# Head of layer 2 in a four-layer graph network: the second batch's turn is queued behind the first batch's products, and the first batch's bias is added by VectorE

## The chip, the core and the metric

The kernel runs on one core of one Trainium2 chip. The metric is the device time of one execution in microseconds (us). TensorE (PE in the profile) multiplies matrices and turns (transposes) them through PSUM, PEld is its loading of weights, VectorE (DVE) and ScalarE (ACT) work elementwise, GpSimd (POOL) does small elementwise work and issues DMAs, and SyncE (SP) issues DMAs.

## The reference

A batch of 16 graphs, each with 1024 nodes and 128 features, goes through four graph layers. After every layer its output is added to the input and each row is normalised. The two lines that matter here are the end of layer 1 and the start of layer 2 (both cut):

```python
# layer 1 ends: h1, h2, h3 are its three batch-normalised hidden states, mf the node mask
xc = jnp.concatenate([h1, h2, h3], axis=-1) * mf[..., None]
y = (xc @ Wl + bl) * mf[..., None]
x = _layernorm(x + y, axis=-1)
# layer 2 begins
h = jnp.einsum('bnf,of->bno', x, W_w) + W_b
e = jnp.einsum('bil,bkl->bik', h @ A, h)
e = e + jnp.swapaxes(e, 1, 2)
att = jax.nn.softmax(jnp.where(adj > 0, e, 0), axis=1) * adj
h_prime = jax.nn.relu(jnp.einsum('bij,bjk->bik', att, h))
```

Layer 2 goes on with gates, a residual sum and a normalisation, and layer 3 is two graph convolutions.

## The kernel before

The program is one long list of tiles. Layers 0 and 1 are done for all batches; layer 1 runs over its batches three times, since its batch norm needs sums over all of them. The change lies where layer 1 has ended and layers 2 and 3 begin (lines 1546 to 1833). From there each batch is worked on in four generator functions: `before` ends layer 1 for this batch and prepares the operands of layer 2, `attention` does the scores, the softmax and the product with the hidden rows in eight steps, `mix` does the gates, and `convolve` does layer 3. A function `in_rounds` lets several of them take turns: each yields a number of rounds that it wants to pause. The first call runs `before` for batches 0 and 1 together, so these two make the head; after that round b runs `attention` of batch b beside `convolve` of b-2, `mix` of b-1 and `before` of b+1.

The order in which the Python code issues instructions isn't yet the order on the engines. A scheduler in the tile framework moves an instruction forward on its engine when it expects its inputs earlier. `keep_in_program_order` ties one instruction behind what was issued last on its engine. Each engine then takes its own queue strictly in order, and an instruction that waits holds up everything behind it on that engine. Buffers come from pools, and a buffer is free again when its last reader is done: `yT` has one buffer (`rows("yT")`), and the PSUM pool `ps_h` has two banks, used in turn by turns and products.

The steps of `before` for one batch, with the lines of the profile:

- L1639: GpSimd multiplies the mask by the bias row `blrow` (named l2A in the profile), 1024 columns wide, into `yT`. `blrow` is ready after L1240, the last step of layer 1's batch norm.
- L1644: TensorE sums the three products of the hidden states with `Wl` into PSUM (`py`).
- L1660: VectorE adds `yT` to each half of `py`, giving `yn`.
- L1664: VectorE adds `yn` to the residual rows `xn`, in two halves for the two batches of the head.
- L794, L796, L742, L745, L799, L801 (`normed`): the statistics on VectorE, the power -1/2 on GpSimd (`ln_rstd`), the shift on VectorE (`ln_nb`), and eight scalings of 128 columns on ScalarE, in two groups of four.
- L1669 with L759 (`turned`): TensorE turns the eight blocks of `xn`, ScalarE copies each half to `xT`.
- L1673 and L1677 with L766 (`products`): `hT` is W2T with `xT`, `G` is As2 with `hT`; each is two products of 512 columns, and ScalarE copies each half out.
- L1680 with L759: TensorE turns `hT`, VectorE copies each half to `hn`.

`attention` then makes scores from `G` and `hT` (L1706, and turned earlier scores at L1708), masks them on VectorE (L1711, `em`), takes the exponential on ScalarE (L1714, `ex`), and multiplies it with the scaled hidden rows `hs` on TensorE (L1694, `acc`).

On the engines of the kernel before, TensorE's queue holds, in this order: the sums of both batches, the turn of batch 0, the turn of batch 1, the four W2T products of both, the As2 products of batch 0, and then turns of hT, score products and the As2 products of batch 1 in alternation. On ScalarE both batches' scalings and xT copies stand ahead of all hT copies.

Of the kernel before, what the change touches and what calls it, by code (L numbers as in the profile page):

```python
# [17 lines left out]
OP = mybir.AluOpType  # L18
# [4 lines left out]
P = 128  # L23
# [616 lines left out]
def fast_kernel(ctx: ExitStack, tc: tile.TileContext, t: dict, out: bass.AP, flag: bass.AP):  # L640

    nc = tc.nc
    B, N, D = t["x"].shape
    NT = N // P
# [6 lines left out]
    identf = consts.tile([P, P], F32, name="identf")  # L651
# [18 lines left out]
    mf = consts.tile([P, BT], F32, name="mf")  # L670
# [57 lines left out]
    def tiles3(ap):  # L728
        return ap.rearrange("p (t d) -> p t d", d=P)

    def per_row(v):

        return v[:, :, None].to_broadcast([P, NT, P])

    def per_col(v):
        return v[:, None, :].to_broadcast([P, NT, P])
# [11 lines left out]
    def halves(psum, tag="h"):  # L748

        for h in range(H2):  # L750
            p = psum.tile([P, 512], F32, name="ph", tag=tag)
            yield p, slice(h * 512, (h + 1) * 512), range(h * 4, h * 4 + 4)

    def turned(psum, src, tag="h"):

        for p, c, blocks in halves(psum, tag):
            for i, k in enumerate(blocks):
                s = src[:, k, :] if len(src.shape) == 3 else src[:, k * P:(k + 1) * P]
                nc.tensor.transpose(p[:, i * P:(i + 1) * P], s, identf)  # L759
            yield p, c, slice(blocks[0], blocks[-1] + 1)  # L760

    def products(psum, *pairs, tag="h"):

        for p, c, _ in halves(psum, tag):
            for i, (W, x) in enumerate(pairs):
                nc.tensor.matmul(p, W, x[:, c], start=(i == 0), stop=(i == len(pairs) - 1))  # L766
            yield p, c
# [19 lines left out]
    def normed(small, r, fine=False, pieces=None):  # L787

        for k in pieces or spans(fine):
            n = k.stop - k.start  # L790
            st = small.tile([P, NT, 6], F32, name="ln_st")
            mv = small.tile([P, NT, 2], F32, name="ln_mv")
            for i in range(n):
                nc.vector.bn_stats(st[:, i, :], r[:, k.start + i, :])  # L794
            for i in range(n):
                nc.vector.bn_aggr(mv[:, i, :], st[:, i, :])  # L796
            rstd = power_mhalf(small, mv[:, :n, 1], add=LN_EPS, name="ln_rstd")
            nb = small.tile([P, NT], F32, name="ln_nb")
            nc.vector.scalar_tensor_tensor(nb[:, :n], mv[:, :n, 0], -1.0, rstd, op0=OP.mult, op1=OP.mult)  # L799
            for i in range(n):  # L800
                nc.scalar.activation(r[:, k.start + i, :], r[:, k.start + i, :], AF.Identity,  # L801
                                     scale=rstd[:, i:i + 1], bias=nb[:, i:i + 1])

    def spans(fine):

        return [slice(0, NT // 2), slice(NT // 2, NT)] if fine else [slice(0, NT)]
# [85 lines left out]
    ps_h = ending.enter_context(tc.tile_pool(name="l0_ph", bufs=2, space=PSUM, reuse_waits="tile"))  # L892

    with tc.tile_pool(name="l0_raw", bufs=1, side="right") as raw:
# [4 lines left out]
        p = ps_h.tile([P, P], F32, name="wtr", tag="h")  # L899
# [3 lines left out]
        p = ps_h.tile([P, P], F32, name="wtr", tag="h")  # L903
# [3 lines left out]
        p = ps_h.tile([P, 1], F32, name="wtr", tag="h")  # L907
# [14 lines left out]
    def before(s, b):  # L922
# [4 lines left out]
        for it in range(NT):  # L927
# [19 lines left out]
            if it == (2 if b else 0):  # L947
                s.xT = work.tile([P, N], F32, name="xT", bufs=2)
                for p, c, _ in turned(ps_h, s.xn):
                    nc.scalar.copy(s.xT[:, c], p)  # L950
# [69 lines left out]

    state = [Batch() for _ in range(B)]
    in_rounds([before(state[0], 0), chain([8], attention(state[0], 0)), chain([16], before(state[1], 1))])
    nc.vector.tensor_scalar(gbh, gb, 0.5, None, op0=OP.mult)
    for b in range(1, B):
        streams = []
        if b < B - 1:
            streams.append(before(state[b + 1], b + 1))
        streams.append(attention(state[b], b))
        if b:
            streams.append(after(state[b - 1], b - 1))  # L1030
        in_rounds(streams)
# [226 lines left out]
    with ExitStack() as ph:  # L1258
# [6 lines left out]
        ps_h = ph.enter_context(tc.tile_pool(name="l1_ph", bufs=4, space=PSUM, reuse_waits="tile"))  # L1265
# [49 lines left out]
        class Step:  # L1315


            def __init__(self, l, before):
                s = str(l + 1)
                self.l = l  # L1320
                self.Wr = matrix(wts, t[f"L1_gnn_Wr{s}"], "Wr", 2)
                self.Wx = matrix(wts, t[f"L1_gnn_Wx{s}"], "Wx", 2)
                self.brow = row_bcast(wts, t[f"L1_gnn_b{s}"], P, "b", 2)
                self.gcol = column(wts, t[f"L1_gnn_g{s}"], f"gcol{s}")
                self.becol = column(wts, t[f"L1_gnn_be{s}"], f"becol{s}")
                self.stats = wts.tile([P, B * H2, 6], F32, name="stats", bufs=2)
                self.batches = [Batch() for _ in range(B)]
                if before is not None:
                    for st, st0 in zip(self.batches, before.batches):
                        st.__dict__.update(st0.__dict__)  # L1330
# [225 lines left out]
    with ExitStack() as ph:  # L1556
# [3 lines left out]
        ps_h = ph.enter_context(tc.tile_pool(name="l2_ph", bufs=2, space=PSUM, reuse_waits="tile"))  # L1560
# [3 lines left out]
        W2T, b2, As2, gw, gb, nbig, blrow, Wl = l2.W2T, l2.b2, l2.As2, l2.gw, l2.gb, l2.nbig, l2.blrow, l2.Wl  # L1564
# [3 lines left out]
        def wide(name, bufs=1, dtype=F32):  # L1568
            return work.tile([P, N], dtype, name=name, bufs=bufs)

        def rows(name, bufs=1, dtype=F32):
            return work.tile([P, NT, P], dtype, name=name, bufs=bufs)
# [60 lines left out]
        def before(s, b):  # L1633

            if b:
                l2.load(s, b)
            yield 2
            yb = rows("yT")
            nc.gpsimd.tensor_tensor(yb, per_row(mf[:, b * NT:(b + 1) * NT]), per_col(blrow), op=OP.mult)  # L1639

            def summed(p, blocks, ls):
                for i, j in enumerate(blocks):
                    for l in ls:
                        nc.tensor.matmul(p[:, i * P:(i + 1) * P], s.hb[l][:, j * P:(j + 1) * P], Wl[:, l, :],  # L1644
                                         start=(l == 0 and (i % 4 == 0 or len(ls) == 3)), stop=(l == 2 and (i % 4 == 3 or len(ls) == 3)))

            if b < 2:

                p = ps_w.tile([P, N], F32, name="py", tag="w")
                for ls in ((0, 1), (2,)):  # L1650
                    summed(p, range(NT), ls)
                turns = [(p[:, h * 512:(h + 1) * 512], range(4 * h, 4 * h + 4)) for h in range(H2)]
            else:
                turns = ((p, blocks) for p, _, blocks in halves(ps_h))
            yn = rows("yn", 1)
            for p, blocks in turns:
                if b >= 2:
                    summed(p, blocks, range(3))
                k = slice(blocks[0], blocks[-1] + 1)
                nc.vector.tensor_add(yn[:, k, :], tiles3(p), yb[:, k, :])  # L1660
            yield 2

            for k in spans(b < 2):
                nc.vector.tensor_add(s.xn[:, k, :], s.xn[:, k, :], yn[:, k, :])  # L1664
            normed(small, s.xn, b < 2)
            yield 6
            s.xT = wide("xT", 2)
            for p, c, _ in turned(ps_h, s.xn):
                nc.scalar.copy(s.xT[:, c], p)  # L1669
            yield 1  # L1670
            s.hT = wide("hT", 2)
            for p, c in products(ps_h, (W2T, s.xT)):
                nc.scalar.activation(s.hT[:, c], p, AF.Identity, bias=b2)  # L1673
            yield 1
            s.G = wide("G", 2)
            for p, c in products(ps_h, (As2, s.hT)):
                nc.scalar.activation(s.G[:, c], p, AF.Copy, scale=-1.0)  # L1677
            s.hn = wide("hn", 2)
            for p, c, _ in turned(ps_h, s.hT):
                nc.vector.tensor_copy(s.hn[:, c], p)  # L1680
            yield
# [200 lines left out]
```

## Time and profile before

| what | value |
|---|---|
| median of 3 runs | 2661.71 us (2660.23 to 2662.22) |
| the profiled execution, its own time | 2657.81 us |
| its span, first to last instruction | 2656.1 us |
| TensorE busy in the span | 2509.0 us (94%) |
| VectorE, ScalarE, GpSimd busy | 2106.4, 1957.0, 356.3 us |
| mean granted TensorE clock | 0.984 of full speed |
| shares of the chain that ended last | PE 53%, DVE 19%, ACT 13%, issue 5%, POOL 4%, DMA 2% |
| L1639 (yT), GpSimd | 16 times, 1.89 us each at the median, first at 1624.2 |
| L1660 (yn), VectorE, halves of the head | 4 times, 0.68 us each |
| L1664 (xn), VectorE, halves of the head | 4 times, 0.68 to 2.38 us, mean 1.53 |
| L1711 (em), first of layer 2 | at 1659.61 |
| L1694 (acc), first of layer 2 | at 1663.79 |

The profile is of one execution. Its times count from the start of its span. A row of the timeline merges instructions of one group that follow each other: start, length from the first start to the last end, engine, line, tiles, count, and in brackets how long the engine was idle before it and what ended that. The ends of matmuls are modelled, about 0.17 us after the array has taken its last column, so busy time of TensorE is on the high side. A float32 product of 512 columns shows as two instructions. "PEclk" is the share of full speed that TensorE's clock was granted.

### The profile page before, as it was taken

To read this page: it belongs to the slowest core of one execution; us is meant where nothing else is said; L and a number is where in the kernel's file an instruction comes from. 1 tells how busy PE (TensorE), PEld (TensorE's weight loads), DVE (VectorE), ACT (ScalarE), POOL (GpSimd) and SP (SyncE) were. 2 spreads that over 40 slices of the span, in tenths; PEclk is the share of its full clock that TensorE was granted. 3 is DMA by queue.
4 is the path that set the end of the run, shared out by engine and by line. 5 is a ranking of instruction groups with operands and counts; after the bars stand their busy time and mean duration, and the time that the engine had idled before them with its cause. 6 is when DMAs were issued, how large, how long until landed. Compare 5 with 4: busy or idle time off the path is not lost.

```text
span 2656.1 us, 44982 instructions
## 1 busy us (share of the span) xinstructions
PE 2509.0 (94%) x16580; PEld 1838.7 (69%) x16584; DVE 2106.4 (79%) x5832; ACT 1957.0 (74%) x3141; POOL 356.3 (13%) x316
## 2 busy tenths in 40 slices
PE   7999999997888869999999998999999999999987
PEld 5777777675666648888888896566666666666655
DVE  5888888887899877777788875777888787887786
ACT  7898898886888866667656534777777777777774
POOL 0001111013000001111122133011111111111001
PEclk9999999998999989999999998999999999999998
DMA  5555555530000052224467582111222111111100
GB/s 195 177 171 176 167 167 183 168 113 21 2 3 2 2 214 96 96 96 146 156 241 249 198 291 105 40 48 65 74 87 70 64 64 64 64 64 64 48 25 26
DMA packets 110103, 285.72 MB, mean 108 GB/s; under 512 B 12080, under 2 KB 53168, under 8 KB 102704
## 3 DMA queue, kind: packets, MB, share of 16 engines
q1 hardware_dynamic: 88832, 197.17, 22.1%
q0 software_dynamic: 21040, 85.57, 9.1%
q8 instruction: 133, 2.18, 0.3%
q14 instruction: 98, 0.80, 0.1%
HBM read 202.85 MB, written 79.82 MB: 106 GB/s over the span
## 4 chain that ended last, share of the span: by engine, by line
PE 53%; DVE 19%; ACT 13%; issue 5%; POOL 4%; DMA 2%; POOLq 0%; ACTq 0%; DVEq 0%; SPq 0%
PE acc L1306 9%; PE ph L1628 8%; PE acc L1694 6%; PE ph L1440 5%; PE ph L759 3%; PE ph L1644 3%; PE acc L973 2%; PE pmm L1706 2%; PE pmm L724 2%; PE ph L1615 2%; ACT em L985 2%; PE ph L766 2%; ACT xn L801 2%; DVE mid L1096 2%; DVE keep L1147 2%
## 5 line engine op out<-in xcount | busy, mean ns | idle before, releaser
L973 PEld LDWEIGHTS acc<-hs,em 128*128 128x128 f32 x2048 | 250.2, 193 | 38.2 <-issue 27.0
L973 PE MATMUL acc<-hs,em 128*128 128x128 f32 x2048 | 270.6, 280 | 0.9 <-DVE hs L989 0.7
L1694 PE MATMUL acc<-ex,hs 128*128 128x512 f32 x512 | 250.3, 599 | 6.2 <-DVE hs L1721 4.1
L724 PE MATMUL pmm<-xT,G 128*128 128x512 f32 x512 | 251.4, 604 | 1.4 <-DVE mx L983 0.7
L801 ACT ACTIVATE xn<-xn,ln_nb,ln_rstd 128x128 f32<-128x128 f32 x512 | 204.8, 480 | 55.3 <-DVE ln_nb L799 55.3
L1306 PE MATMUL acc<-a,hi 128*128 128x512 f32 x768 | 235.0, 398 | 3.0 <-ACT hi L1272 3.0
L1306 PE MATMUL acc<-a,lo 128*128 128x512 f32 x768 | 228.3, 392 | 3.1 <-DVE lo L1273 3.1
L745 POOL TENSOR_TENSOR ln_rstd<-ln_rstd,mhalf 128x8 f32<-128x8 f32 (+1 forms) x69 | 107.9, 1564 | 806.1 <-DVE ln_rstd L742 452.2
L1714 ACT ACTIVATE ex<-em,mn 128x1024 f32<-128x1024 f32 x128 | 146.6, 1145 | 89.2 <-DVE mn L1711 85.9
L983 DVE CUSTOM_DVE_ANT_0 em<-pmm,msk 128x1024 f32<-128x1024 f32 x128 | 155.9, 1218 | 35.5 <-PE pmm L724 33.2
L985 ACT ACTIVATE em<-em,mx 128x1024 f32<-128x1024 f32 x128 | 146.0, 1141 | 48.0 <-DVE mx L983 46.4
L1706 PE MATMUL pmm<-G,hT 128*128 128x512 f32 (+3 forms) x416 | 171.4, 520 | 0.1
L1306 PEld LDWEIGHTS acc<-a,lo 128*128 128x128 f32 x768 | 142.9, 188 | 34.0 <-DVE lo L1273 4.5
L1306 PEld LDWEIGHTS acc<-a,hi 128*128 128x128 f32 x768 | 140.7, 188 | 33.6 <-ACT hi L1272 3.7
L1156 ACT ACTIVATE carry<-pc,negone 128x1024 fp8e4<-128x1024 f32 x128 | 141.4, 1116 | 27.0 <-PE pc L1155 24.3
L1711 DVE CUSTOM_DVE_ANT_0 em<-pmm,msk 128x1024 f32<-128x1024 f32 x128 | 155.2, 1213 | 2.3 <-PE pmm L1708 0.6
L931 ACT ACTIVATE carry<-an 128x1024 fp8e4<-128x1024 f32 x128 | 134.1, 1049 | 24.5 <-DMA an<-in_adj 23.7
L980 ACT ACTIVATE msk<-carry,l0nbig 128x1024 bf16<-128x1024 fp8e4 x128 | 145.9, 1139 | 0.0
L1702 ACT ACTIVATE msk<-A,nbig 128x1024 bf16<-128x1024 fp8e4 x128 | 144.1, 1136 | 0.0
L1628 PE MATMUL ph<-A,hi 128*128 128x512 f32 x512 | 143.7, 422 | 0.2 <-ACT hi L1618 0.2
L1694 PEld LDWEIGHTS acc<-ex,hs 128*128 128x128 f32 x512 | 87.4, 189 | 78.6 <-issue 52.8
L1295 ACT CAST a<-carry 128x1024 fp32r<-128x1024 fp8e4 x96 | 98.9, 1047 | 43.4 <-PE acc L1306 43.2
(315 smaller groups left out, 6214.0 us busy)
## 6 DMA issues: line engine op xcount, KB each, us to landing
an<-in_adj SPq DMA_DIRECT2D x128, 512.0 KB, 4.1
adj_d<-carry POOLq DMA_DIRECT2D x16, 1024.0 KB, 4.6
A<-dil_d SPq DMA_DIRECT2D x16, 1024.0 KB, 6.0
rdeg<-rdeg_d SPq DMA_DIRECT2D x32, 512.0 KB, 4.6
A<-adj_d SPq DMA_DIRECT2D x16, 1024.0 KB, 4.8
ag_d<-ag POOLq DMA_DIRECT2D x24, 512.0 KB, 5.7
ag<-ag_d SPq DMA_DIRECT2D x24, 512.0 KB, 5.8
x_d<-xn POOLq DMA_DIRECT2D x16, 512.0 KB, 3.9
```

Source lines behind the costliest of these rows:

```text
L724: nc.tensor.matmul(p[:, h * 512:(h + 1) * 512], lhsT, rhs[:, h * 512:(h + 1) * 512], start=True, stop=True)
L801: nc.scalar.activation(r[:, k.start + i, :], r[:, k.start + i, :], AF.Identity, scale=rstd[:, i:i + 1], bias=nb[:, i:i + 1])
L973: nc.tensor.matmul(s.acc[:, c], em[:, c], hs, start=(jt == 0 and k % 4 == 0), stop=(jt == NT - 1 and k % 4 == 3))
L980: nc.scalar.activation(msk, Y[b][:, jt, :], AF.Identity, scale=-BIG, bias=nbig)
L983: nc.vector.tensor_tensor_reduce(em, e, msk, 1.0, 3.0e38, op0=OP.add, op1=OP.min, accum_out=mn)
L985: nc.scalar.activation(em, em, AF.Exp, scale=-1.0, bias=mn, accum_out=sm)
L1306: nc.tensor.matmul(acc, part[:, jt, :], pieces[h * NT // 2 + k][:, jt - 2 * k, :], start=(part is parts[0] and jt == 0), stop=(part is par ...
L1628: nc.tensor.matmul(p, part[:, jt, :], A[jt][:, c], start=(jt == 0 and i == 0), stop=(jt == NT - 1 and i == 1))
L1694: nc.tensor.matmul(s.acc[:, c], hs, ex[:, c], start=(jt == 0), stop=(jt == NT - 1))
L1706: nc.tensor.matmul(e[:, c], s.hT[:, js], s.G[:, c], start=True, stop=True)
L1711: nc.vector.tensor_tensor_reduce(row, e, msk, 1.0, 0.0, op0=OP.add, op1=OP.min, accum_out=mn)
L1714: nc.scalar.activation(ex, row, AF.Exp, scale=-1.0, bias=mn, accum_out=sm)
```

## The change

Three edits, all in the head. `turned` gets a switch that ties the first block of the turn behind what was issued last on TensorE, and `before` sets it for batch 1. Batch 1 pauses nine rounds instead of six after its normalisation is issued, so in program order its turn comes after the first batch's products. And for batch 0 the GpSimd product is left out; VectorE instead makes each block of yn from the bias row, the mask's column and the PSUM block, in eight instructions of 128 columns.

```diff
-    def turned(psum, src, tag="h"):
+    def turned(psum, src, tag="h", behind=False):
 
         for p, c, blocks in halves(psum, tag):
             for i, k in enumerate(blocks):
                 s = src[:, k, :] if len(src.shape) == 3 else src[:, k * P:(k + 1) * P]
-                nc.tensor.transpose(p[:, i * P:(i + 1) * P], s, identf)
+                turn = nc.tensor.transpose(p[:, i * P:(i + 1) * P], s, identf)
+                if behind and k == 0:
+                    tc.keep_in_program_order(turn)
             yield p, c, slice(blocks[0], blocks[-1] + 1)
...
             yb = rows("yT")
-            nc.gpsimd.tensor_tensor(yb, per_row(mf[:, b * NT:(b + 1) * NT]), per_col(blrow), op=OP.mult)
+            if b:
+                nc.gpsimd.tensor_tensor(yb, per_row(mf[:, b * NT:(b + 1) * NT]), per_col(blrow), op=OP.mult)
...
                 k = slice(blocks[0], blocks[-1] + 1)
-                nc.vector.tensor_add(yn[:, k, :], tiles3(p), yb[:, k, :])
+                if b:
+                    nc.vector.tensor_add(yn[:, k, :], tiles3(p), yb[:, k, :])
+                else:
+                    for i, j in enumerate(blocks):
+                        nc.vector.scalar_tensor_tensor(yn[:, j, :], blrow, mf[:, j:j + 1], p[:, i * P:(i + 1) * P],
+                                                       op0=OP.mult, op1=OP.add)
...
             normed(small, s.xn, b < 2)
-            yield 6
+            yield 9 if b == 1 else 6
             s.xT = wide("xT", 2)
-            for p, c, _ in turned(ps_h, s.xn):
+            for p, c, _ in turned(ps_h, s.xn, behind=b == 1):
                 nc.scalar.copy(s.xT[:, c], p)
```

On the engines this changes the order within the head alone. On TensorE the turn of batch 1 now stands behind batch 0's four products, its hT turn and two of the first score products. On ScalarE batch 0's hT copies and the first half of its G stand ahead of batch 1's scalings, the second half of G behind them. On VectorE both hn copies of batch 0 still stand behind batch 1's last `ln_nb`. GpSimd has one product less, and SyncE's queue is the same. The changed lines move the later ones by two to eight: L1664 becomes L1672, L1711 becomes L1719, L766 becomes L768.

## The prediction

> **What bounds the head now.** All instants below are us from the start of the profiled execution (span 2656.1, its own time 2657.81, so 1.7 lie outside the span; the median of the runs shown is 2661.71, 3.9 above that execution, so I carry over only a difference). I read the chain of work that ended last first, between 1600 and 1700. Its pieces are start, length, work:
>
> ```profile
> 1627.86 2.90 DVE xn L1664 x2
> ...
> 1636.53 2.90 DVE xn L1664 x2
> ...
> 1644.71 1.63 PE ph L759 x4
> 1646.34 8.25 PE ph L766 x12
> ```
>
> The chain runs through VectorE twice, once for each batch (residual sum L1664, then normalisation), and reaches TensorE only with the second batch's turn at 1644.71. The timeline of all engines shows the sums (start, length, engine, line, operation; in brackets the idle time before it and what ended that):
>
> ```profile
> 1627.78 2.98 DVE L1664 TENSOR_TENSOR xn<-xn,yn 128x512 f32<-128x512 f32 x2
> ...
> 1628.01 2.21 POOL L1639 TENSOR_TENSOR yT<-mf,l2A 128x1024 f32<-128x1024 f32 x1 [1.91 <-DVE yn L1660]
> ...
> 1630.68 0.86 DVE L794 BATCH_NORM_STATS2 ln_st<-xn 128x6 f32<-128x128 f32 x4
> ```
>
> and that of TensorE alone shows the queue:
>
> ```profile
> 1635.91 1.48 PE L759 MATMUL ph<-identf,xn 128*128 128x128 f32 x4 [0.49 <-ACT xn L801]
> 1642.60 1.63 PE L759 MATMUL ph<-identf,xn 128*128 128x128 f32 x4 [5.21 <-ACT xn L801]
> 1644.71 1.63 PE L759 MATMUL ph<-identf,xn 128*128 128x128 f32 x4 [0.48 <-ACT xn L801]
> 1646.33 6.35 PE L766 MATMUL ph<-xT,l2WT 128*128 128x512 f32 x8
> ```
>
> TensorE ends the first batch's turn at 1637.4. Next in its queue stands the second batch's turn, so it idles 5.21 and is then paced by ScalarE until 1646.33, although the first batch's xT was copied by 1638. Every product of the first batch is queued behind that. The windows view, cut at 3.41 us (each row: length, busy time of PE, PEld, DVE, ACT, POOL, then PEclk), gives the second loss:
>
> ```profile
> 1634.63:1638.04 3.41, 2.05 (x8) 0.83 (x6) 2.87 (x5) 3.07 (x8) 1.87 (x2) 1.00 0.93 356
> 1638.04:1641.46 3.42, 0.00 (x0) 0.00 (x0) 3.08 (x13) 0.00 (x0) 1.49 (x2) 0.50 0.05 22
> 1641.46:1644.87 3.41, 1.79 (x5) 0.89 (x5) 0.97 (x8) 2.36 (x6) 1.37 (x2) 0.50 0.00 0
> 1644.87:1648.28 3.41, 3.41 (x7) 1.48 (x8) 0.00 (x0) 1.99 (x5) 0.00 (x0) 0.50 0.01 2
> 1648.28:1651.70 3.42, 3.42 (x6) 1.26 (x5) 0.00 (x0) 1.37 (x2) 0.00 (x0) 0.50 0.00 0
> 1651.70:1655.11 3.41, 3.41 (x12) 1.43 (x11) 0.01 (x1) 2.46 (x4) 0.00 (x0) 1.00 0.00 0
> ```
>
> TensorE's clock falls to half at 1638.04 and comes back at 1651.70: four windows. The eight passes of the first four products take 6.26 (1646.33 to 1652.59) where at full clock a pass of 512 columns takes 0.43 (0.86 for the two of L1706 in the chain).
>
> **Part 1, the bias (L1639, L1660).** Removed: one GpSimd product of 1.9 and two VectorE sums, 1.29 together. Added: eight 128x128 scalar_tensor_tensor from PSUM, back to back. No such row exists; four 128x128 bn_stats take 0.86 (above), one alone about 0.27, so a step is (0.86-0.27)/3 = 0.20: eight are 1.69, or 0.40 more. At worst each costs its full 0.29 (the single 128x128 sum L1240): 2.3, or 1.0 more. Below nothing is excluded: the same 1024 columns with six more starts. I take 0.4. What it frees is larger. The first batch no longer uses yT, whose only buffer made the second batch's GpSimd product wait until 1628.01, on top of the first batch's xn sums. There a 128x512 sum took 2.38 instead of 0.68 (L1664: shortest 681 ns, longest 2384), since it ended with GpSimd's. In the changed order that product stands right behind the bias, 1624.2 to 1626.1, before VectorE's first block at 1626.57. So the two sums take 1.24 of issue, not 2.90: -1.66. Net -1.26 for the first batch's normalisation. The second batch keeps its collision (the third batch's yT still waits for its yn, L1660 at 1635.25). If the cover of 1624.2 to 1626.1 failed, the 1.7 would come back.
>
> **Part 2, the pin.** [...] Step by step at full clock, first batch: L801 starts at 1633.40-1.26 = 1632.1 and ends near 1635.8; the turn ends at 1635.9 (before 1637.4; TensorE is on the second batch's sums until 1634.4, which delays only its first half). xT copies to 1636.9; the W2T products start near 1636.4 (before 1646.33); As2 to 1639.9; hT turn, then two score halves to 1642.1. Now the new waits. The second hT turn needs the bank that the first hn copy empties, and that copy is queued on DVE behind the second batch's ln_nb. The second batch's yn starts when its sums end, 1634.4 instead of 1635.25, so that ln_nb moves from 1643.96 to about 1643.1; copy and turn end at 1644.5. Then the pinned turn waits for the second G half, which is queued on ACT behind the second batch's L801 (1644.16 before, 1643.4 now, +1.65, +0.6): 1645.7. Behind it wait the second score half, the first mask step on DVE (before 1659.61, now about 1647.7) and the whole first attention.
>
> Sum, in lost TensorE time. Before: 5.21 idle, plus 3.73-0.88 = 2.85 in the paced turn (eight of 0.11 inside 1642.60 to 1646.33), plus 6.26-3.44 = 2.8 at half clock: 10.9. After: 0.4 (xT) + 1.9 (1642.1 to 1644.0) + 1.2 (1644.5 to 1645.7) = 3.5. Gain 7.4, and 1.3 from part 1, since the turn ends that much earlier: **8.7 if the clock stays full**.
>
> It probably doesn't. [...] The row of 1634.63:1638.04 says otherwise: PE is busy for 2.05 of 3.41, no gap in it passes 0.7, and the clock falls at its end. The changed kernel has about 0.8 of score product and 0.5 of turn between 1641.46 and 1644.87, less than that. So I take the row: the clock falls at some edge from 1644.3 to 1647.0 and returns after the first window filled throughout, one or two windows later, 3.41 or 6.83 at half speed, 1.7 or 3.2 of lost work as TensorE is then dense: **gain 7.0 or 5.5**. Edges lie on a 3.41 grid that the program doesn't set; moving it over the rows of before costs that kernel 0 to 2 more than in this execution (a half-clock stretch of five windows, where this one has four), 0.7 on average. Likeliest gain: 6.25+0.7 = 6.9, so 2661.7-6.9 = **2654.8**.
>
> Nothing later takes it back in the profile: after 1650 PE is busy and on the chain through L1694, L1644 and L1628, DMA share is near 0 until 1690, and the second batch's G (now about 1653) is needed first at about 1671.
>
> **Rivals.**
> *Clock stays full.* The grid puts an edge near 1644, which splits the two gaps (about 0.7 of 3.41, 20%). Gain 8.7 to 9.4, 2652.6.
> *Gain mostly lost: within 0.2%* (5.3 us, about what a measurement of this kernel tells from no change). The clock stays at half for three windows or more, as before (13.65), because the pieces after 1645.7 wait for ACT. Another 1.7: gain 3.8, 2657.9. Or the half-clock stretches near the end (four such windows between 2583 and 2604) fall worse by one or two once everything shifts.
> *Slower.* The pin makes the first attention wait for the second batch's normalisation through ACT's queue: G's second half and the turn stand behind all eight L801. In the sum these end at 1645.1. Each us later costs one us, as nothing but that turn may run. It decides once they end over 7 later; slower by 0.2% needs 12 later, near 1657. The longest delay in the trace here is the 1.7 sum beside GpSimd, so five of them in a row; price then 2667.
> *The bias change does nothing for the sums:* if the eight blocks cost 0.29 each and still meet GpSimd, part 1 is +1.0, not -1.26, and the gain 4.7, 2657.0.
>
> **Numbers.** Clock falls for one or two windows, gain 5.5 to 8: 0.58. Stays full, over 8: 0.17. Within 0.2%, of the third and fourth kind: 0.21. Slower: 0.04. The first case's low end overlaps the bound a little, so faster 0.73, same 0.23, slower 0.04. Range: from the full clock with 1.5 for the runs' own spread (2660.23 to 2662.22), 2651.3, to the half-lost case, 2658.5.
>
> **What would show it.** Right: the second GpSimd yT gone from beside the first batch's xn sums, those at 0.68 each; L766 beginning near 1636.4 at PEclk 1.00; gaps of about 1.9 and 1.2 on PE before the pinned turn, released by DVE hn and ACT G; the first L1711 near 1647.7 and L1694 9 earlier than 1663.79 less the clock's share; everything after shifted alike. Wrong: PEclk at 0.50 from 1638, eight blocks over 2 us, or the shift shrinking between 1700 and the end.

## The result and the profile after

| | before | after |
|---|---|---|
| median | 2661.95 us (22 runs) | 2657.07 us (22 runs) |
| profiled execution, its own time | 2657.81 us | 2655.82 us |
| its span | 2656.1 us | 2654.0 us |

The ratio is 0.998, with a 95% interval of 0.9974 to 0.9987: 3.5 to 6.9 us less, 4.9 between the medians. The forecast was 6.9 less (2654.8), with a range of 2651.3 to 2658.5. The time lies in that range, but 4.9 is under the 5.5 to 8 of its likeliest case and falls among the gains within 0.2% (5.3 us), which it gave 0.21.

The chain of work that ended last, after (start, length, work):

```profile
1627.55 4.31 DMA hb<-h1T_d
1631.90 6.97 PE py L1647 x46
...
1647.81 1.65 ACT xn L803 x4
1649.46 0.49 ACT G L1685
1649.99 1.97 PE ph L759 x8
```

The first batch has left this part of the chain. What runs through it is the second batch alone: its hidden states arrive, its sums are made, it is normalised, it holds ScalarE's queue in front of the first batch's second G half, and the pinned turn follows. TensorE's own timeline shows what that does to its queue:

```profile
1639.97 1.98 PE L768 MATMUL ph<-xT,l2WT 128*128 128x512 f32 x4 [0.24 <-ACT xT L1677]
...
1644.18 1.88 PE L1714 MATMUL pmm<-G,hT 128*128 128x512 f32 x4
1648.57 0.90 PE L759 MATMUL ph<-identf,hT 128*128 128x128 f32 x4 [2.51 <-DVE hn L1688]
1649.99 1.97 PE L759 MATMUL ph<-identf,xn 128*128 128x128 f32 x8 [0.53 <-ACT G L1685]
```

The W2T products start right behind the first batch's turn and xT copy, and no longer wait for the second batch's turn. The 5.21 of idle time is gone, and the two waits named in the forecast stand in its place, with the releasers that it named: 2.51 (VectorE's hn) and 0.53 (ScalarE's G). The windows view, cut every 3.41 us, at the edges on which each change of the clock in this execution's record stands (length, busy time of PE, PEld, DVE, ACT, POOL, then PEclk, the DMA share and GB/s):

```profile
1628.36:1631.77 3.41, 1.25 (x9) 0.86 (x8) 2.61 (x9) 0.00 (x0) 0.38 (x1) 1.00 0.92 356
1631.77:1635.19 3.42, 3.29 (x15) 3.29 (x16) 2.68 (x16) 0.04 (x1) 1.02 (x1) 0.50 0.23 91
...
1645.43:1648.84 3.41, 0.90 (x4) 0.28 (x3) 1.67 (x9) 2.67 (x7) 1.05 (x2) 1.00 0.00 0
1648.84:1652.25 3.41, 2.88 (x13) 2.32 (x12) 0.69 (x1) 1.94 (x5) 0.00 (x0) 0.50 0.00 0
```

The clock is at half in two single windows, not four in a row. Each follows a window in which TensorE was busy for 1.25 or 0.90. The first of them falls on the second batch's sums, where the clock of before stayed full.

The bias, in the timeline of all engines:

```profile
1626.84 1.90 POOL L1642 TENSOR_TENSOR yT<-mf,l2A 128x1024 f32<-128x1024 f32 x1 [2.31 <-DVE l2A L1242]
...
1629.16 2.16 DVE L1667 SCALAR_TENSOR_TENSOR yn<-l2A,mf,py 128x128 f32<-128x128 f32 x8 [2.39 <-PE py L1647]
1631.23 1.29 DVE L1672 TENSOR_TENSOR xn<-xn,yn 128x512 f32<-128x512 f32 x2
```

GpSimd's product for the second batch ends at 1628.7, ahead of the first block, and the xn sums take 1.29 instead of 2.98. The eight blocks take 2.16 where the two sums took 1.29.

### The profile page after: what moved, and what is told of

Its sections match the earlier page's. It is cut to its first block, busy times and chain, and to the rows that moved or that the text cites. A ratio compares the mean times of both kernels' runs of the same rounds, so it can differ in the third digit from the quotient of the medians.

```text
span 2654.0 us, 44987 instructions
## 1 busy us (share of the span) xinstructions
PE 2508.8 (95%) x16584; PEld 1839.2 (69%) x16584; DVE 2106.6 (79%) x5838; ACT 1956.5 (74%) x3141; POOL 354.4 (13%) x315
## 3 DMA queue, kind: packets, MB, share of 16 engines
q1 hardware_dynamic: 88832, 197.17, 22.2%
## 4 chain that ended last, share of the span: by engine, by line
PE 50%; DVE 19%; ACT 14%; issue 6%; POOL 4%; DMA 3%; POOLq 0%; ACTq 0%; DVEq 0%; SPq 0%
PE acc L1308 9%; PE ph L1630 8%; PE acc L1702 6%; PE ph L1442 4%; PE ph L1647 3%; PE ph L759 3%; ACT xn L803 2%; PE pmm L1714 2%; PE pmm L724 2%; ACT em L987 2%; PE ph L1617 2%; PE acc L975 2%; PE ph L768 2%; DVE mid L1098 2%; DVE keep L1149 2%
## 5 line engine op out<-in xcount | busy, mean ns | idle before, releaser
L1719 DVE CUSTOM_DVE_ANT_0 em<-pmm,msk 128x1024 f32<-128x1024 f32 x128 | 155.3, 1214 | 8.2 <-PE pmm L1714 5.3
L933 ACT ACTIVATE carry<-an 128x1024 fp8e4<-128x1024 f32 x128 | 134.1, 1049 | 25.3 <-DMA an<-in_adj 24.6
```

Source lines behind the costliest of these rows:

```text
L1719: nc.vector.tensor_tensor_reduce(row, e, msk, 1.0, 0.0, op0=OP.add, op1=OP.min, accum_out=mn)
```

## The experiments

All kernels were timed beside before. To compare the heads of different executions I count from the first yn, since what lies ahead of it is the same code and its start moves between 1626.6 and 1632.5 from one profile to another. "Half" is the number of 3.41 us windows at half clock between the first yn and the ninth mask step (L1711 of before), all in us. Where two kernels share the order behind the head, the ninth and the thirty-third mask step give the same difference; where they don't, the thirty-third is the one to go by:

| kernel | ratio to before (95%) | second batch's sums end | W2T starts | first mask step | ninth | 33rd | half |
|---|---|---|---|---|---|---|---|
| before | 1 | 8.0 | 19.75 | 33.0 | 55.63 | 224.94 | 4 |
| after | 0.9980 (0.9974 to 0.9987) | 9.7 | 10.8 | 23.9 | 49.66 | 218.97 | 2 |
| e9, after again | 0.9982 (0.9975 to 0.9988) | 9.7 | 10.8 | 23.9 | 49.66 | 218.99 | 2 |
| e1, bias only | 0.9998 (0.9990 to 1.0006) | 8.2 | 19.3 | 31.7 | 54.26 | 223.57 | 3 |
| e2, pin only | 0.9980 (0.9970 to 0.9990) | 9.8 | 11.0 | 24.6 | 50.35 | 219.69 | 2 |
| e3, after with filling | 0.9972 (0.9963 to 0.9982) | 8.5 | 10.1 | 21.6 | 47.37 | 216.69 | 0 |
| e5, pin with filling | 0.9975 (0.9968 to 0.9983) | 8.2 | 11.0 | 21.8 | 47.52 | 216.88 | 0 |
| e6, the same, own bias tile | 0.9972 (0.9961 to 0.9982) | 8.0 | 9.3 | 22.2 | 48.61 | 217.92 | 1 |
| e8, before with 7 fillings | 1.0003 (0.9995 to 1.0011) | 9.7 | 20.9 | 33.4 | 55.97 | 225.27 | 3 |
| e12, before, clock full | 0.9987 (0.9978 to 0.9996) | 8.2 | 19.75 | 30.6 | 53.17 | 222.49 | 0 |
| e4, queues cleared | 0.9958 (0.9945 to 0.9970) | 8.2 | 10.1 | 17.1 | 46.40 | 213.94 | 0 |
| e10, VectorE's queue put back | 0.9974 (0.9965 to 0.9982) | 9.9 | 11.0 | 20.1 | 48.99 | 218.35 | 2 |
| e7, e4 with filling, own bias tile | 0.9953 (0.9939 to 0.9966) | 8.1 | 9.3 | 17.0 | 46.38 | 213.95 | 0 |
| e11, e4 with filling, both biases on VectorE | 0.9959 (0.9946 to 0.9973) | 8.1 | 10.1 | 16.8 | 44.67 | 214.06 | 0 |

Some expectations count to the ninth mask step from the batch norm instead: e1 and e2 from its aggregate, where before has 61.5 and the change 56.2; e5 to e8 from the last step of its scale some 2.4 later, where e3 has 50.8 and before 59.1. These counts take in some of the clock ahead of the head: from the aggregate to the first yn it is 5.8 to 6.0 where the half-clock stretch there ends 4.8 or more ahead of the first yn, and 6.4 to 6.5 where it ends later. So the counts from the first yn decide.

### The two parts alone: e1 and e2

e1 leaves out the pin and the longer pause:

```diff
-            yield 9 if b == 1 else 6
+            yield 6
-            for p, c, _ in turned(ps_h, s.xn, behind=b == 1):
+            for p, c, _ in turned(ps_h, s.xn):
```

> Only the first batch's bias is moved to VectorE (eight 128x128 blocks); the second batch's turn stays where it was on TensorE, ahead of the first batch's products. Theory (the queue on TensorE is what the change pays for, the bias only shortens the first batch's normalisation): every product of the first batch still waits for the second batch's turn, so only what the second batch gains counts: its yn starts when its sums end instead of behind the first batch's ln_nb, 0 to 0.9 us less than before; TensorE's gap ahead of the second batch's turn stays over 4 us. The time from the batch norm's aggregate to the ninth mask step is 60.6 to 61.5 where before has 61.5 and the full change 56.2. Rival (the bias is half of the gain): 1.3 to 2.5 us less than before.

Measured: 0.9998, 60.25 from the aggregate. TensorE's gap ahead of the second batch's turn is 5.59, and W2T starts 0.44 earlier after the first yn than in before. The rest of the 1.37 at the ninth mask step goes with one half-clock window less. So the bias alone brings nothing that the time can show (1.6 slower to 2.7 faster). That leaves room for the rival's 1.3 to 2.5; it is the trace, with 0.44 ahead of the W2T products, that speaks against it.

e2 gives the first batch its GpSimd product and two sums back:

```diff
-            if b:
-                nc.gpsimd.tensor_tensor(yb, per_row(mf[:, b * NT:(b + 1) * NT]), per_col(blrow), op=OP.mult)
+            nc.gpsimd.tensor_tensor(yb, per_row(mf[:, b * NT:(b + 1) * NT]), per_col(blrow), op=OP.mult)
...
-                if b:
-                    nc.vector.tensor_add(yn[:, k, :], tiles3(p), yb[:, k, :])
...
+                nc.vector.tensor_add(yn[:, k, :], tiles3(p), yb[:, k, :])
```

> Only the pin and the longer pause of the second batch; the first batch's bias is again one GpSimd product and two VectorE sums. Theory: nearly the whole gain of the full change, 3.5 to 5 us less than before; the first batch's xn sum beside GpSimd takes 2.4 again and the turn of the first batch comes 0.8 to 1.3 later than with the full change; from the aggregate to the ninth mask step 56.5 to 58. Rival (the pin pays only because the bias made the first batch early): under 2.5 us less than before.

Measured: 0.9980, as much as the full change. The 56.19 from the aggregate, where the full change has 56.16, isn't the same head: from the first yn, e2 has 50.35 and the full change 49.66, 0.69 later. The first scaling comes 6.83 after the first yn (full change 5.99), yet W2T starts only 0.15 later: in both, TensorE ends the second batch's sums at half clock only 9.7 to 9.8 after the first yn, and the first batch's turn stands behind these sums. Here the half clock covers what the bias edit won: 0.84 at the first scaling, 0.15 at W2T. Of the 0.69, 0.11 stands at the pinned turn; the rest comes with the second half-clock window, which begins 21.0 after the first yn here and 19.7 in the full change, over denser work.

### The clock: e3, e5, e8, e12

e3 keeps TensorE busy while it waits for the second batch's hidden states, with three products into a bank that is overwritten later:

```diff
+        def warmed(n, last):
+            with tc.issue_after(last.ins):
+                idle = ps_a.tile([P, N], F32, name="acc")
+                for _ in range(n):
+                    last = nc.tensor.matmul(idle[:, :3 * P], identf, Wl.rearrange("p l d -> p (l d)"), start=True, stop=True)
+            return last
...
+                    if b == 1:
+                        order.enter_context(tc.issue_after(warmed(3, state[0].last).ins))
```

> The full change, and three products of 384 columns with the unit matrix into the still unused accumulator bank (0.65 us each, results overwritten) in the 2.3 us in which TensorE waits for the second batch's hidden states, ahead of its sums. Theory (the clock that falls there halves the speed of the second batch's sums, which then set its chain): those sums take 5.4 instead of 6.95, the second batch's yn starts 1.3 to 1.8 earlier after the first batch's yn, the gap of 2.51 ahead of the second hT turn shrinks to about 1; 1 to 2 us less than the full change in an execution where that clock falls, so about 5.5 to 7 less than before. Rival (VectorE is the bound: the second batch's yn waits for the first batch's last ln_nb anyway, and the clock falls there only in some executions): no more than 0.5 less than the full change.

TensorE's timeline of e3:

```profile
1629.14 2.10 PE L1574 MATMUL acc<-Wl,identf 128*128 128x384 f32 x6
...
1632.44 5.40 PE L1654 MATMUL py<-Wl,hb 128*128 128x128 f32 x46 [0.79 <-DMA hb<-h1T_d]
```

The sums take 5.40 where after has 6.95, the second half-clock window is gone as well, and the ninth mask step comes 2.29 earlier than after. The gap ahead of the second hT turn shrinks to 1.98, not to 1: it is set by the second batch's normalisation, which starts when the sums end. In the time, 7.4 less than before stands against 4.9; the intervals overlap (4.8 to 9.8 and 3.5 to 6.9), so the trace decides here, not the medians.

e5 is e3 with the edit of e2: the pin alone, at full clock.

> The pin alone, with the three filling products ahead of the second batch's sums; the first batch's bias by GpSimd and two VectorE sums as before. With the filling the clock stays full over the second batch's sums, so the first batch's turn waits for its own scalings and no longer for these sums. Theory (what ends the head is the second batch's normalisation, which starts when its sums end, so the bias edit buys nothing): from the aggregate to the ninth mask step within 0.4 of the run with bias, pin and filling (50.8), although the first batch's scalings come 0.8 later after its yn. Rival (the bias edit is worth its 0.8 to 1.3 once the clock no longer hides it): 51.5 to 52.2, and 0.8 to 1.3 us slower.

Measured: 50.99 against 50.78, and 47.52 against 47.37 from the first yn. The first batch's scalings come 0.83 later and W2T too (10.96, 10.13), but the first mask step only 0.14. What takes up the difference is TensorE's wait ahead of the second hT turn, in e5 and then in e3:

```profile
1646.12 0.66 PE L759 MATMUL ph<-identf,hT 128*128 128x128 f32 x4 [1.28 <-DVE hn L1692]
```

```profile
1647.55 0.65 PE L759 MATMUL ph<-identf,hT 128*128 128x128 f32 x4 [1.98 <-DVE hn L1698]
```

So with the clock out of the way the bias edit is still worth only 0.15: the second batch's normalisation, which starts with the end of its sums, is what is late, and TensorE waits for it 0.70 longer when the first batch is 0.83 earlier.

e8 tried to price the half clock in before with seven such products in the 5.21 gap, ahead of the second batch's turn.

> The kernel before with seven filling products of 384 columns (4.6 us at full clock) in the 5.21 us in which TensorE waits ahead of the second batch's turn. The order is that of before. Theory (half the clock over the first four products costs 2.8): PEclk stays 1.00 from 1638 on, the eight passes of W2T take 3.5 instead of 6.3, from the aggregate to the ninth mask step 56.0 to 57 instead of 59.1, 2 to 3 us less than before. Rival (the fall comes with the paced turn behind the filling, or TensorE isn't the bound there): 0 to 1 us less.

It didn't answer: the clock fell at 1632.03 over the second batch's sums, and again behind the filling at 1645.68, after a window with 1.56 of busy time (a rest of the gap, 1.79, and the paced turn). W2T took 5.65. e12 fills the paced turn as well, with nine products and one of 128 columns behind each of the eight blocks:

```diff
+                if idle is not None:
+                    with tc.issue_after(state[0].turn.ins):
+                        state[0].turn = nc.tensor.matmul(idle[:, :P], identf, identf, start=True, stop=True)
```

> The kernel before with nine filling products of 384 columns ahead of the second batch's turn and one of 128 columns behind each of its eight blocks, so that TensorE streams through the whole wait and the paced turn. Theory (the run with seven products failed to keep the clock, because the turn itself, eight blocks of 0.11 in 3.7 us, is too thin): PEclk stays 1.00 from the first batch's turn to the first mask step, the eight passes of W2T take 3.5 instead of 6.3, the ninth mask step comes 52.8 to 53.6 after the first yn instead of 55.6, and 2 to 3 us less than before. That would be the share of the clock in what before loses; the rest to the full change with filling (47.4) is the order on TensorE. Rival (behind the turn something else is the bound, as the second batch's xT or the bank): 54.5 or more with the clock full.

TensorE's timeline of e12:

```profile
1641.91 5.97 PE L1578 MATMUL acc<-Wl,identf 128*128 128x384 f32 x18
...
1651.00 3.89 PE L772 MATMUL ph<-xT,l2WT 128*128 128x512 f32 x8
```

W2T takes 3.89 where before has 6.35, at the same start after the first yn (19.75), and the ninth mask step comes 2.46 earlier, as expected. This splits the head: from e12 to e5 only the pin and its pause are new, both at full clock: 53.17 to 47.52.

### The two queues that are left: e4 and e10

e4 issues the second batch's normalisation after the first batch's operands and ties it there (its scalings behind the second G copy, its last ln_nb behind the hn copies, its turn behind the first score product):

```diff
+            with ExitStack() as order:
+                if behind:
+                    order.enter_context(tc.issue_after(behind.gcopy.ins))
+                    if k.start:
+                        order.enter_context(tc.issue_after(behind.hncopy.ins))
...
+                if b == 1:
+                    order.enter_context(tc.issue_after(state[0].score.ins))
...
-        in_rounds([before(state[b], b) for b in range(2)])
-        for b in range(B - 1):
+        in_rounds([chain(before(state[0], 0), attention(state[0], 0)), before(state[1], 1)])
+        for b in range(1, B - 1):
```

> The full change, but with the second batch's normalisation behind the first batch's operands also on the other two engines: ScalarE copies both halves of the first G ahead of the second batch's eight scalings, VectorE copies hn ahead of the second batch's last ln_nb, and the second batch's turn stands behind both halves of the first score product. Theory (what the change leaves is lost in those two queues, in order: 2.51 ahead of the second hT turn, 0.53 behind it, and the first mask step waiting for the turn): the first mask step comes 20 us after the first yn instead of 23.9, TensorE has no gap over 1 ahead of it, and the time is 2 to 4 us below the full change, 7 to 9 below before. Rival (TensorE's own work is the bound behind 1650, and a wait for the mask step and the exponential takes the place of the gaps): less than 1 us below the full change.

VectorE's timeline of e4:

```profile
1643.44 1.29 DVE L1699 COPY hn<-ph 128x512 f32<-128x512 f32 x2
...
1644.71 1.22 DVE L1732 CUSTOM_DVE_ANT_0 em<-pmm,msk 128x1024 f32<-128x1024 f32 x1
```

The first mask step follows the hn copies at once, 17.1 after the first yn where after has 23.9. The time is 8.0 to 14.6 below before, apart from the changed kernel's 3.5 to 6.9. Of the 6.8 at the first mask step, 5.03 are left at the thirty-third. Part of that is the clock, which stays full in e4: against e3, also at full clock, e4 has 4.5 at the first and 2.75 at the thirty-third. So the two queues were worth 2.75. That is what the two waits of e3 add up to (1.98 and 0.77), and in e4 both are gone: from 11 to 50 us after the first yn TensorE is idle for 0.51 in all, where e3 has 2.92. An earlier first mask step alone is no TensorE time. Against the changed kernel as it is, the gain is more than the 2 to 4 expected (5.03 in the profiles, 10.6 below before between the medians where 7 to 9 were expected), as the clock comes on top.

e10 takes back VectorE's part alone (the two lines with `hncopy`).

> The order of e4 with one thing taken back: VectorE copies hn behind the second batch's last ln_nb again; ScalarE still copies both halves of the first G ahead of the second batch's scalings, and the second batch's turn still stands behind both halves of the first score product. Theory (both queues hold the head, one behind the other): the second hT turn waits again for hn, about 2 us on TensorE, but behind it the first mask step comes at once instead of behind the second batch's turn: 19 to 19.8 us after the first yn, between e4 (17.1) and the full change (21.6 with filling, 23.9 without); the median 1 to 2.5 slower than e4. Rival (one of the queues is all of it): 17.1 if it was ScalarE's, over 21 if it was VectorE's.

TensorE's timeline of e10:

```profile
1652.20 1.12 PE L759 MATMUL ph<-identf,xn 128*128 128x128 f32 x7 [2.16 <-DVE hn L1697]
```

TensorE waits 2.16 for hn again, and the first mask step comes 20.1 after the first yn, between the two and a little behind the 19 to 19.8 expected. The clock is at half for two windows, as in after, so after is the one to compare with: 3.8 earlier at the first mask step, but only 0.6 at the thirty-third. So most of what e4 brings needs VectorE's queue cleared as well. The time is 4.8 to 9.3 below before, not told apart from after.

### Who was in the way of the xn sums, and is there more: e6, e7, e9, e11

e6 is e5 with a tile of its own for the first batch's bias:

```diff
-            yb = rows("yT")
+            yb = rows("yT") if b else work.tile([P, NT, P], F32, name="yT0", tag="x3T", bufs=1)
```

> As the run before, but GpSimd writes the first batch's bias into a tile of its own (the space of a tile that is first used in layer 3), so that its second product need not wait for the first batch's yn: the first batch has two sums of 512 columns and no GpSimd beside its xn sums. Theory (the shared buffer, not who adds the bias, made the xn sum slow): yn 1.29 instead of 2.16 and xn 1.29 instead of 2.98, the first scaling 0.87 earlier after the first yn than with the eight blocks (5.1 instead of 6.0); the aggregate to the ninth mask step still within 0.4 of 50.8, since the second batch's chain sets it. Rival (GpSimd's second product still meets the sums, or the earlier start counts): first scaling at 6 or later, or the head 0.9 shorter.

The first scaling comes 5.17 after the first yn, with yn 1.29 and xn 1.32: two sums beat eight blocks by 0.8 once the buffer isn't shared. The edit's gain on the xn sums is the freed buffer, not VectorE. The ninth mask step is off the expectation (52.6 from the scale, 48.61 from the first yn); this profile has a half-clock window behind the gap ahead of the second hT turn. The time is that of e5.

> The order of e4 (both queues cleared ahead of the second batch), the filling products, and the first batch's bias by GpSimd into a tile of its own. Theory: with both queues cleared the first batch's own chain is what is late, so here its 0.87 counts: 48.9 from the aggregate to the ninth mask step where e4 has 49.8; the clock cannot fall ahead of the second batch's sums. 10.5 to 13 us less than before. Rival (TensorE's work is dense from the first batch's products on, and is the bound together with the second batch's sums that stand ahead of its turn): no less than e4, 9.5 to 11 less than before.

By the trace the rival was right, no less than e4: W2T starts 0.84 earlier than in e4, but the first mask step comes only 0.1 earlier and the thirty-third at the same time. The time can't tell the two: it is 9.1 to 16.2 below before, which takes in the 10.5 to 13 of the theory and the 9.5 to 11 of the rival. What sets the first mask step, though, is VectorE's queue: VectorE makes the first hn copies only behind the second batch's statistics, 15.7 after the first yn here and 15.8 in e4.

> The changed kernel once more, unaltered, beside before on the same chip as the next two, and for a second profile. Theory (the gain of the change in this execution depends on where TensorE's clock windows fall): the median again 3.5 to 7 below before; from the first yn to the ninth mask step 49.7 as in the first profile if the clock falls ahead of the second batch's sums and in the gap ahead of the second hT turn, 48.5 if it falls in one of the two, 47.4 (as in the runs with filling) if in neither; the gap ahead of the second hT turn 2.0 to 2.5. Rival (the half clock isn't what separates the first profile from the runs with filling): 49.5 or more with the clock full over the head.

The two half-clock windows and all landmarks repeat to 0.03. The edges of the windows stand at the same distance from the first yn as in the first profile (the first half-clock window begins 2.61 behind it in both), so this is a repetition and says nothing of other positions.

> The order of e4 and the filling products, and the second batch's bias as well by VectorE in eight blocks, so that GpSimd's next product needs no buffer that the second batch reads and no longer runs beside the second batch's xn sums; the planner's order behind the head shifts somewhat. Theory (in e4 and e7 the first mask step is late because VectorE has the second batch's sums and statistics ahead of it): the second batch's xn sums take 1.29 instead of 2.98, its yn 2.16 instead of 1.29, so the first mask step 0.5 to 0.8 earlier after the first yn (16.3 to 16.6 where e4 and e7 have 17.1 and 17.0), and the median 0 to 1 below e7. Rival (TensorE is dense there and is the bound): the first mask step earlier but the ninth not.

The first mask step comes 0.2 earlier, not 0.5. The ninth is 1.7 earlier, but the thirty-third (214.06) no earlier than in e4 (213.94) and e7 (213.95), nor is the time. The rival had the ninth no earlier either, which isn't so, but it is right in what it says of the bound: the lead is gone by the thirty-third.

## Why the prediction was right, and where its sum was off

The mechanism was right: the order on TensorE, two new waits in its place, the clock as a tax on both kernels. The gain was over-estimated by 2.0 of 6.9. In the profiles the head gains 5.97, inside the likeliest case; the median's 4.9 is within 0.2%, but not by a half clock of three windows or more, nor by the stretches near the end, the reasons that the forecast gave for "gain mostly lost". The rival "the bias change does nothing for the sums" has the number (gain 4.7, 2657.0) by chance: the bias edit does add almost nothing, but its blocks cost 0.26 and not 0.29, they don't meet GpSimd's product, and the sums do get faster. Two of the three signs of being wrong did come: eight blocks over 2 us, and a shift that shrinks before the end.

**The lost TensorE time (10.9 to 3.5).** Without the clock the sum said 5.21 + 2.85 less 3.5, and 1.3 from the bias: 5.9. Measured, at full clock on both sides: 53.17 - 47.37 = 5.80. But it is made up differently, and that the sums agree is luck. The pin gives 5.65 (e12 to e5) where the sum has 4.6, the bias 0.15 (e5 to e3) where it has 1.3. The gaps that remain at full clock are 1.98 and 0.77 with the bias edit and 1.28 and 0.77 without it; the forecast had 1.9 and 1.2.

**Part 1, "and 1.3 from part 1, since the turn ends that much earlier": this step failed.** Its terms were roughly right. The xn sums fell by 1.69 (forecast 1.66), and GpSimd's product had ended before the first block. The blocks were mis-sized: 0.26 apart, not 0.20 as the bn_stats row suggested, so 2.16 in all and +0.87 instead of +0.40, within the bound of +1.0. Net: the first scaling comes 0.83 earlier. What failed is the step from there to the end. The same paragraph hung the pinned turn on the second batch's scalings, and these start from its own sums, which the bias doesn't touch. A turn that ends earlier only makes the next wait longer: by 0.70 of 0.83 (e5 and e3).

**The clock.** "2.8 at half clock" in before is 2.46 (e12). After, the forecast was one window or two in a row, at an edge of 1644.3 to 1647.0, 1.7 or 3.2. Shifted by the first yn's 2.6, the edge at 1648.84 is inside, and it was one window: 1.1, by e6 against e5. That the clock returns after the first window filled throughout, from which the forecast had its one or two, is shown by no run: in before the window from 1644.87 was filled (3.41 of 3.41) and the next one still ran at half, and in after the clock came back behind windows with 3.29 and 2.88. The other window was not foreseen: at 1631.77, over the second batch's sums, about 1.2 as the rest of 2.29 (e3 against after). Together they are the middle of what was taken, by luck, since one of the two places was not the one foreseen. The row of before, from which the forecast took that the clock falls, was borne out, but it gives no threshold: the clock fell there at 2.05 of busy time, all of it turns, and in after at 1.25 (gaps of 1.50 and 0.79) and 0.90 (a gap of 2.51), while windows of products stayed at full clock at 1.78 and 2.04 (e1, e4).

So the head gains 5.80 + 2.46 - 2.29 = 5.97 between the profiles (55.63 to 49.66), where the text had 6.25.

**"Nothing later takes it back": this step failed too.** The lead stays within 5.9 to 6.0 up to the ninety-ninth mask step and drops by 1.76 at the next, near 2360; 0.43 of that comes back at the one after, so 1.3 is lost. VectorE waits there for a later batch's residual rows, in before and then in after:

```profile
2358.81 1.21 DVE L1664 TENSOR_TENSOR xn<-xn,yn 128x1024 f32<-128x1024 f32 x1
```

```profile
2357.14 1.23 DVE L1672 TENSOR_TENSOR xn<-xn,yn 128x1024 f32<-128x1024 f32 x1 [1.68 <-DMA xn<-x_d]
```

DMA queues and transfers of the 10 us around it, before:

```profile
q8 instruction: 1, 0.02, 0.6%
...
xn<-x_d SPq DMA_DIRECT2D x1, 512.0 KB, 4.0
```

and after:

```profile
q8 instruction: 1, 0.02, 1.2%
...
xn<-x_d SPq DMA_DIRECT2D x1, 512.0 KB, 6.1
```

The load is issued 2.69 ahead of the ninety-ninth mask step in both, and needed 4.4 after its issue. It lands after 4.0 in before and after 6.1 in the changed kernel. With it in the window stands a fetch of instructions (queue q8), which takes twice as long (1.2% of sixteen engines' 10 us is 1.9, against 1.0). The load lands after 5.3 to 6.1, and costs 0.6 to 1.3, in the profiles of after, e9, e2, e4 and e10; in before and the other eight kernels it lands after 4.0 or 4.1. Those five have the pin and no filling. The times of the single packets tell them apart. In the five, the fetch starts 1.2 to 2.6 behind the issue of the load, so it falls into the transfer; in the other nine it starts at least 0.4 ahead of the issue and is over before the load's first packet. In the nine, all 1024 packets of the load (512 bytes each) have started by 3.5 behind the issue. In after, where the fetch runs from 2.07 to 3.93, 43 of them start later than 3.7, the last at 5.4; in the other four it is 15 to 52. So the load lands late (5.3 to 6.1 against 4.0 or 4.1) where a fetch falls into it. That the fetch holds it up is read from fourteen profiles that agree; no run moved the fetch alone, and what moves it is open. The rival "stretches near the end" named another place: half-clock windows between 2580 and 2604 rose from four to six in after, but from the last mask step to the end of the span the lead changes by only 0.04 (by 0.5 in e9).

**The 0.7 for other grid positions** can't be told; no run shows this term. The traces show the grid: counted from the start of the span, every change of the clock stands at a whole number of 3.413 plus 3.06 in before and plus 0.20 in after, though the code up to the head is the same. What the head of before costs at another position they don't show. The 0.7 should have made the medians differ by more than the profiles. From the first yn to the end of the span the profiles differ by 5.97 - 1.32 = 4.65, and the medians by 4.9; with the 0.7 it would be 5.35, which the interval of 3.5 to 6.9 takes in as well. From the 6.9 to the 4.65 of the profiles it is these 0.7, the 1.3 at the load and 0.3 in the head.

**Marks.** W2T at full clock, 10.8 after the first yn (forecast 9.8). The first mask step at 23.9 (forecast 21.1 at full clock; e3, 21.6). First acc product 6.6 earlier after the first yn (9 less the clock's share). The rival "slower" found nothing: the second batch's scalings ended at 1649.5, 4.4 later than forecast, 2.6 of which is the later start of the head.

## What to carry to other kernels

Before a shortened step is counted as gain, name what is late next; here the sum held the pinned turn to the second batch and still credited the first batch's head start. When one queue is reordered, look at the same two batches on every other queue: the change moved the second batch back on TensorE alone, and clearing ScalarE's and VectorE's queues as well (e4) gave another 2.75 in the head at full clock. A load that lands 0.4 us before it is needed is a cost that a change of code far away can call in (1.3 us here, some 700 us later).

## What was not expected of the hardware

TensorE waits for the second batch's hidden states in both kernels (1.47 and 0.76 in before, 1.50 and 0.79 in after), and without filling there the clock fell at this wait in some profiles and stayed full in others: the window that takes in this wait had a busy time of 1.21, 1.25, 1.62, 1.70 or 1.72 where the clock fell at its end (e9, after, e2, e8, e10), and 1.78, 2.04 and 2.50 where it stayed (e1, e4, before). Three products that nobody needs, 2.1 us in such a wait, kept these sums at 5.40 (e3, e5, e6, e7) instead of 6.95 (after).

A fetch of instructions that fell into a load of 512 KB went with a landing after 5.3 to 6.1 us; the same load landed after 4.0 or 4.1 where the fetch came ahead of it.
